# A MetaFormer block on one Trainium2 core: quarter-tile mixing, a column-tiled transform along w, unstrided scaling and one bias addition

## The chip, the cores and the metric

The kernel runs on one core of one Trainium2 chip. The metric is the device time of one execution in microseconds. The kernel before took 2752.03 us, the median of two runs (2751.84 and 2752.21 us).

## What is computed

The input x is 8 images of 128 x 128 points (h, w) with 96 channels, in fp32. One layer is applied to it:

```python
x = x + conv(_ln_c(x))            # layer norm over the 96 channels, then conv
t = x as tokens
t = t + ffn(_ln_t(t))             # layer norm again, then a quantised MLP
# conv(x), per image, with MED = 192 and a half spectrum of 128 x 65:
x_pre = scale * relu(x @ w1.T) ** 2 + bias
xf = rfft2(x_pre over h, w)                        # "ortho"
r = softmax over 3 filters of a small MLP of the image's means
comb = sum_s filt[s] * r[s]                        # complex, resized from small tables
out = irfft2(xf * comb) @ w2.T                     # 192 -> 96 channels
# ffn: 96 -> 384 -> 96, products in fp8 (5 exponent bits), sums rounded to fp16
y = q16(q8(x) @ q8(W1).T);  h = relu(q16(y + q8(b1)));  out = q16(q16(q8(h) @ q8(W2).T) + q8(b2))
```

## The kernel before, in words

Both Fourier transforms are matrix products. Work on image b is cut into three streams. Stream "a" (`before`, lines 622 to 827) goes over w in 32 units of 4 columns, and normalises, projects (96 to 192 + 48), rectifies, squares, transforms along h and stores the rows to DRAM. Stream "s" (`spectrum`, lines 829 to 1102) goes over 33 groups g of spectrum rows: it transforms along w, multiplies by the filter of the image, goes back to a real basis, mixes 192 channels into 96 for a pair p of groups, and inverts along w; there are 16 pairs. Stream "c" (`after`, lines 1104 to 1258) goes over w in 32 units again: last inverse transform along h, residual, layer norm, the fp8 MLP, output. Three images are in work at once, one in each stream.

The order of the instructions is fixed when the program is built. Every step is entered with `at(time, what, ..., after=..., banks=...)`: a time from tables written out by hand (`STREAMS`, `O`, `OWN`), the steps that it needs, and how many of six PSUM banks it takes. `in_order` (line 323) is a list scheduler that turns this into one order, and lines 1285 to 1295 pin each engine's instructions to it. So each engine, and each of the queues that issue DMAs (SP's and ACT's), works strictly in that order, and a step that is late holds up what stands behind it.

The steps that the change touches are these.

- **Scaling.** `load_xT` (644) brings 8 columns of x, transposed, as [96, h, 8]; `load_r` (652) brings 1/std as [h, 8], spread over 96 partitions; `scale` (656) multiplies 4 columns at a time into one of three buffers `zTs`, reading both inputs with a step of 8 elements. `project` (669) uses the result as stationary operand.
- **Transform along w.** `pack` (859) on POOL gathers the last 64 channels of two rows into one 128-column operand. `along_w` (868) then does three fp32 products of 128 rows x 128 columns against 130 columns; it is called twice for a group (cs = 0 and 1).
- **Filters.** `filters_of` (878) does twelve products of 52 rows x 64 columns, placed so that four lie in different quarters of TensorE's array; for the last group (g = 32) only the upper row half is used, six products.
- **Mixing.** `mix_low` (963) opens two banks with four bf16 products by zero (971), then adds sixteen 64 x 64 products for the third 64 channels (984). `mix` (992) adds eight 128 x 128 products (995). `mixed` and `invert` (1003, 1008) take the result out and transform it.
- **MLP.** `accumulated` (1174) copies 512 columns of a product to fp16 on ACT; `biased` (1179) adds b1 and clips at zero on DVE, once for each of three chunks; `hidden` (1183) casts all 1536 elements to fp8 on ACT.
- **Stream c's loads.** `load_v` (1112) brings x to a tile `xr`; `residual` (1127) writes the sum to a tile `t`, of which there are four.

Of the kernel before, what the change touches and what calls it, by code (L numbers as in the profile page):

```python
# [44 lines left out]
MED = 192  # L45
# [222 lines left out]
def _columns(p, r):  # L268

    if p < NP - 1:  # L270
        return [(g, cs) for g in (2 * p, 2 * p + 1) for cs in range(2)]
    return [(NG - 1, 0), (NG - 1, 1)] + [(NG, 0), (NG, 1)] * (r == 0) + [(NG + 1, 0)]
# [98 lines left out]
def metaformer_kernel(ctx: ExitStack, tc: tile.TileContext, a: dict, out: bass.AP):  # L371
    nc = tc.nc
    x, xT = a["x"], a["xT"]
# [49 lines left out]
    zeros = const.tile([128, 64], mybir.dt.bfloat16, name="zeros")  # L423

    NZT = 3
    zTs = [const.tile([C + 1, QW, 128], F32, name=f"zT{i}") for i in range(NZT)]
# [8 lines left out]
    w2A = load(T_CONST, "w2A", [128, C], a["w2T"][:128, :])  # L435
    w2B = const.tile([128, C], F32, name="w2B")
# [4 lines left out]
    b1q = const.tile([128, NHC], F32, name="b1q")  # L441
# [3 lines left out]
    def projection(sp):  # L445
# [36 lines left out]
        def others():  # L482
            for i in range(2):
                nc.sync.dma_start(out=w2B[64 * i : 64 * i + 64, :], in_=a["w2T"][128:, :])
            make_identity(nc, ident)
            nc.vector.tensor_copy(ident8, ident, saturate=False)
            nc.vector.memset(ones, 1.0 / (H * W))
            nc.vector.memset(zeros, 0.0)

            nc.vector.tensor_scalar(soa_bias, soa_bias, 128.0, None, ALU.mult)  # L490
# [6 lines left out]
    def filters(sp):  # L497
# [38 lines left out]
        def weights():  # L536
# [15 lines left out]
            nc.vector.tensor_copy(b1q, b1h)  # L552
# [69 lines left out]
    def before(b, t0, P):  # L622
# [4 lines left out]
        one = named("a", b, {None: NU, **dict.fromkeys(blocks, NWB), "load_xT": NU // 2, "load_r": NU // 2})  # L627
# [4 lines left out]
        def load_x(blk):  # L632
            if blk == 0:
                kept["gacc"] = pa.tile([C, NU], F32, name="gacc", tag="gacc")
            xb = pa.tile([128, WB, C], F32, name="xb", tag="xb")
            nc.sync.dma_start(out=xb, in_=x[b, :, blk * WB : (blk + 1) * WB, :])
            kept["x", blk] = xb
# [6 lines left out]
        def load_xT(hb):  # L644
            t = kept["xT", hb] = pa.tile([C, H, HB], F32, name="xT", tag="xT")
            nc.sync.dma_start(out=t, in_=xT[b, hb, :, :, :])

        def store_r(blk):
            t = kept["Rd", blk] = dram.tile([2, H, HB], F32, name="Rd", tag="Rd")
            nc.sync.dma_start(out=t.rearrange("f h w -> h f w"), in_=kept["r", blk].rearrange("h (f w) -> h f w", f=2))  # L650

        def load_r(hb):
            t = kept["rB", hb] = pa.tile([C, H, HB], F32, name="rB", tag="rB")
            nc.sync.dma_start(out=t, in_=kept["Rd", hb // 2][hb % 2].partition_broadcast(C))

        def scale(u):
            hb, q = divmod(u, 2)
            w = slice(q * QW, (q + 1) * QW)
            nc.vector.scalar_tensor_tensor(  # L659
                zTs[(b * NU + u) % NZT][:C, :, :],  # L660
                kept["xT", hb][:, :, w].rearrange("c h w -> c w h"),
                1.0,
                kept["rB", hb][:, :, w].rearrange("c h w -> c w h"),
                ALU.mult,
                ALU.mult,
                accum_out=kept["gacc"][:, u : u + 1],
            )

        def project(u, i0):
            px = kept["px", u, i0] = bank("px")[:, : 2 * (MED + SCTX)]  # L670
            for i in range(2):
                nc.tensor.matmul(  # L672
                    px[:, i * (MED + SCTX) : (i + 1) * (MED + SCTX)],
                    lhsT=zTs[(b * NU + u) % NZT][:, i0 + i, :],
# [42 lines left out]
        for u in range(NU):  # L717
            t = t0 + u * P
            blk, q = divmod(u, NQ)
            if q == 0:  # L720
# [3 lines left out]
                at(t + o["a_store_r"] * P, store_r, blk, after=[one("rest", blk)])  # L724
            if q % 2 == 0:
                hb = u // 2
                after = [one("scale", u - 4 + n) for n in (0, 1)]
                at(t + o["a_load_xT"] * P - 3, load_xT, hb, after=after)
                at(t + o["a_load_r"] * P, load_r, hb, after=after + [one("store_r", blk)])
            at(t + o["a_measure"] * P, measure, blk, q, after=[one("load_x", blk), one("rest", blk - 2)])  # L730
            after = [one("load_xT", u // 2), one("load_r", u // 2)] + both("project", u - NZT)
            at(t + o["a_scale"] * P, scale, u, after=after)
            for i0 in (0, 2):
                after = [one("scale", u), one("square", u - 2), one("context", u - 2)]
# [88 lines left out]
        after = [one("context", NU - 1), one("scale", NU - 1)]  # L823
# [5 lines left out]
    def spectrum(b, t0, P):  # L829
# [29 lines left out]
        def pack(g):  # L859

            yb = kept["yb", g] = psp.tile([128, 2, 2, 64], F32, name="yb", tag="yb")
            yt = kept["yt", min(g, NG)]
            src = yt[:, :, 128:].rearrange("w (s k) m -> w s k m", s=2)
            if g == NG:
                src = yt[:, 0:2, 128:].unsqueeze(2).to_broadcast([128, 2, 2, 64])
            nc.gpsimd.tensor_copy(yb, src)

        def along_w(g, cs):
            yt, yb = kept["yt", min(g, NG)], kept["yb", g]
            ja, jb = (2 * cs, 2 * cs + 1) if g < NG else (cs, cs) if g == NG else (2, 3)  # L870
            both = yb[:, 1 if g > NG else cs, :, :].rearrange("w k m -> w (k m)")
            pz = kept["pz", g, cs] = bank("pz")
            for u, y in enumerate((yt[:, ja, :128], yt[:, jb, :128], both)):
                nc.tensor.matmul(  # L874
                    pz[:, u * 2 * L : (u + 1) * 2 * L], lhsT=y, rhs=F2[:, cs, :], start=True, stop=True
                )

        def filters_of(g):
# [3 lines left out]
            halves = [(u, h, u * MED + 64 * h) for u in range(2) for h in range(2)]  # L882
            halves += [(2, k, k * MED + 128) for k in range(2)]
            for u, h, m0 in halves:
                for s in range(2 if g <= NG else 1):
                    p = slice(64 * s, 64 * s + R)
                    nc.tensor.matmul(  # L887
                        pf[64 * h : 64 * h + 64, s, u * 2 * L : (u + 1) * 2 * L],
                        lhsT=tb[p, m0 : m0 + 64],
                        rhs=RW[p, :],  # L890
                        start=True,
                        stop=True,
                    )
# [53 lines left out]
        def alone_t(g):  # L947
            z = kept["dm", g]
            nc.vector.tensor_tensor(z[:, 0, 0, 0:1], z[:, 0, 0, 0:1], soa_bias, ALU.add)
            nc.vector.tensor_tensor(z[:64, 2, 0, 0:1], z[:64, 2, 0, 0:1], soa_bias[:64], ALU.add)  # L950
# [12 lines left out]
        def mix_low(p):  # L963

            for r in range(2):
                kept["pv", p, r] = bank("pv")
            for h in range(2):
                for r in range(2):
                    half, rows = slice(64 * h, 64 * h + 64), slice(64 * r, 64 * r + 64)
                    n = len(_columns(p, r)) * C  # L970
                    nc.tensor.matmul(
                        kept["pv", p, r][half, :n],
                        lhsT=zeros[rows, :64],
                        rhs=zeros[rows, :1].to_broadcast([64, n]),
                        start=True,
                        stop=False,
                    )
            for i in range(5):
                for h in range(2):
                    for r in range(2):  # L980
                        if i < len(_columns(p, r)):
# [4 lines left out]
                                lhsT=kept["xf", g][rows, cs, 2, half],  # L986
                                rhs=w2B[rows, :],
                                start=False,
                                stop=False,
                            )  # L990

# [343 lines left out]
```

## Time and profile before

| what | value |
|---|---|
| two runs | 2751.84 and 2752.21 us |
| profiled execution: span from first to last instruction | 2754.4 us (no other time of this execution is recorded) |
| mean granted TensorE clock | 0.970 |
| PE / PEld / DVE / ACT / POOL busy | 93 / 71 / 83 / 81 / 77% of the span |
| DMA | 618.05 MB, mean 224 GB/s |
| PE, DVE, ACT, POOL busy from 500 to 1000 us | 492.16, 445.01, 429.79, 426.42 us |
| PE, DVE, ACT, POOL busy from 2610 to 2755 us | 88.57, 108.11, 123.78, 44.13 us |
| DVE: `biased` (L1181), 768 times | 427.5 us, 568 ns each |
| DVE: `scale` (L659), 256 times | 339.8 us, 1328 ns each |
| POOL: `pack` (L866), 264 times | 138.5 us, 525 ns each |
| ACT: `hidden` (L1185), 256 times | 386.2 us, 1509 ns each |
| DVE: bias of the second layer (L1207), 64 times | 67.4 us, 1054 ns each |

PE is TensorE's matmuls, PEld its weight loads, DVE the VectorE, ACT the ScalarE, POOL the GpSimd, SP a queue that issues DMAs. A group's line gives source line, engine, operation, "out<-in" by tile names, shapes, count, then busy time and the mean duration of one instruction. Busy time on PE is a union of overlapping instructions, so the start times of successive groups, in the timeline, say more on TensorE than busy time does. An fp32 product appears as two matmul records.

### The profile page before, as it was taken

What the parts mean: (1) busy time and instruction counts of PE and PEld (TensorE: products, weight loads), DVE (VectorE), ACT (ScalarE), POOL (GpSimd) and SP (SyncE); (2) the same over time, 40 slices, a digit from 0 to 9 for tenths busy, and PEclk for the clock granted to TensorE, in tenths of its full rate; (3) what the DMA queues carried; (4) which work ended last, traced back from release to release, by engine and by line L of the source; (5) the groups of instructions that cost most, each with busy time, mean ns of one, the idle gap of its engine ahead of it and who ended that gap; (6) DMA issues with size and microseconds to landing.
All of it is one profiled execution on the core that took longest, in us unless ns stands there. A gap on an engine that the chain in (4) does not pass through costs nothing.

```text
span 2754.4 us, 69406 instructions
## 1 busy us (share of the span) xinstructions
PE 2567.8 (93%) x25130; PEld 1953.0 (71%) x25130; DVE 2276.1 (83%) x5887; ACT 2233.0 (81%) x4452; POOL 2122.2 (77%) x3246
## 2 busy tenths in 40 slices
PE   4989999999999999999999999999999998999765
PEld 2668877777677777777677777777777776677433
DVE  3557667798898999889898889889889878999786
ACT  2665556699888879889998878889988997888898
POOL 1239997888788878988688969888788886889432
PEclk9899999999999999999999999999999998999896
DMA  7888777977688866878687757888777774656441
GB/s 205 263 263 253 242 224 241 287 233 251 209 255 260 252 213 196 271 242 262 220 258 245 243 171 220 273 259 257 231 239 242 230 222 147 185 178 190 149 129 62
DMA packets 480023, 618.05 MB, mean 224 GB/s; under 512 B 174542, under 2 KB 381270, under 8 KB 479658
## 3 DMA queue, kind: packets, MB, share of 16 engines
q1 hardware_dynamic: 424386, 462.60, 56.8%
q10 hardware_dynamic: 55296, 151.02, 14.7%
q8 instruction: 199, 3.26, 0.5%
q14 instruction: 142, 1.16, 0.1%
HBM read 405.36 MB, written 208.16 MB: 223 GB/s over the span
## 4 chain that ended last, share of the span: by engine, by line
PE 68%; DVE 13%; ACT 7%; POOL 4%; DMA 4%; issue 3%; SPq 1%; POOLq 0%; ACTq 0%; DVEq 0%
PE px L672 13%; PE pz L874 10%; PE py L701 10%; PE pv L995 7%; PE pf L887 6%; PE pg L1011 5%; PE ph L1170 4%; PE pk L1123 4%; PE po L1192 3%; PE pv L984 3%; DVE t L916 3%; DVE y L1181 2%; ACT h L1185 2%; ACT y L1177 2%; DVE st L581 2%
## 5 line engine op out<-in xcount | busy, mean ns | idle before, releaser
L923 POOL TENSOR_TENSOR rr<-t,t 128x390 f32<-128x390 f32 x512 | 520.4, 1017 | 60.4 <-DVE t L916 60.0
L672 PE MATMUL px<-W1S,zT 97*128 97x240 f32 x2048 | 519.4, 379 | 34.1 <-DVE zT L659 29.2
L1177 ACT CAST y<-ph 128x512 f16<-128x512 f32 x768 | 456.0, 603 | 24.2 <-PE ph L1170 22.4
L672 PEld LDWEIGHTS px<-W1S,zT 97*128 97x128 f32 x2048 | 377.2, 194 | 130.0 <-issue 33.7
L1151 ACT ACTIVATE z<-t,ln_m,ln_r 128x96 fp8e5<-128x96 f32 x960 | 461.2, 492 | 8.6 <-POOL ln_m L614 5.7
L1181 DVE TENSOR_SCALAR y<-y,b1q 128x512 f16<-128x512 f16 x768 | 427.5, 568 | 28.2 <-ACT y L1177 25.6
L683 ACT ACTIVATE rl<-px 128x480 f32<-128x480 f32 x512 | 295.7, 581 | 177.5 <-PE px L672 160.2
L701 PE MATMUL py<-X,F 128*128 128x384 f32 x1024 | 430.7, 507 | 2.1 <-ACT X L690 1.9
L1185 ACT ACTIVATE h<-y 128x1536 fp8e5<-128x1536 f16 x256 | 386.2, 1509 | 2.2 <-DVE y L1181 1.6
L659 DVE SCALAR_TENSOR_TENSOR zT<-xT,rB 96x512 f32<-96x512 f32 x256 | 339.8, 1328 | 53.1 <-DMA rB<-Rd 26.5
L874 PEld LDWEIGHTS pz<-F,yt 128*128 128x128 f32 x2080 | 301.4, 192 | 72.0 <-DVE t L1131 5.9
L1210 POOL TENSOR_TENSOR t<-t,o 128x1536 f32<-128x1536 f32 x64 | 210.1, 3282 | 167.8 <-DVE o L1207 165.8
L874 PE MATMUL pz<-F,yt 128*128 128x130 f32 x2080 | 329.0, 281 | 10.2 <-DVE t L1131 4.7
L857 POOL TENSOR_TENSOR tb<-tb,r 128x384 f32<-128x384 f32 (+1 forms) x264 | 287.0, 1087 | 59.7 <-DVE r L808 23.1
L916 DVE TENSOR_TENSOR t<-dm,pf 128x390 f32<-128x390 f32 x512 | 282.6, 552 | 43.8 <-PE pf L887 18.4
L1170 PE MATMUL ph<-zT,W1q 96*128 96x512 fp8e5 x768 | 293.5, 397 | 19.1 <-DVE zT L1166 13.9
L708 ACT COPY yst<-py 128x384 f32<-128x384 f32 x512 | 246.4, 486 | 74.3 <-PE py L701 67.8
L916 DVE TENSOR_TENSOR t<-dp,pf 128x390 f32<-128x390 f32 x512 | 280.3, 548 | 0.0
L940 POOL TENSOR_TENSOR xf<-rr 128x378 f32<-128x378 f32 x256 | 255.3, 997 | 19.7
L995 PEld LDWEIGHTS pv<-w2A,xf 128*128 128x128 f32 x2048 | 246.8, 194 | 13.6 <-issue 1.5
L995 PE MATMUL pv<-w2A,xf 128*128 128x96 f32 x2048 | 255.2, 278 | 0.0
L938 POOL TENSOR_TENSOR xf<-rr 128x390 f32<-128x390 f32 x256 | 250.1, 977 | 0.0
(126 smaller groups left out, 5210.5 us busy)
## 6 DMA issues: line engine op xcount, KB each, us to landing
Yd<-yst ACTq DMA_DIRECT2D x256, 384.0 KB
yt<-Yd SPq DMA_DIRECT2D x256, 384.0 KB
xb<-in_x SPq DMA_DIRECT2D x64, 768.0 KB
xT<-in_xT SPq DMA_DIRECT2D x128, 384.0 KB
rB<-Rd SPq DMA_DIRECT2D x128, 384.0 KB
tb<-T SPq DMA_DIRECT2D x256, 192.0 KB
Vd<-gst ACTq DMA_DIRECT2D x128, 384.0 KB
xr<-in_x SPq DMA_DIRECT2D x64, 768.0 KB
```

The costliest lines, as they stand in the source:

```text
L659: nc.vector.scalar_tensor_tensor(zTs[(b * NU + u) % NZT][:C, :, :], kept["xT", hb][:, :, w].rearrange("c h w -> c w h"), 1.0, kept["rB", h ...
L672: nc.tensor.matmul(px[:, i * (MED + SCTX) : (i + 1) * (MED + SCTX)], lhsT=zTs[(b * NU + u) % NZT][:, i0 + i, :], rhs=W1S, start=True, stop ...
L701: nc.tensor.matmul(py, lhsT=F1, rhs=kept["X", u][:, i0 : i0 + 2, :].rearrange("h w m -> h (w m)"), start=True, stop=True)
L874: nc.tensor.matmul(pz[:, u * 2 * L : (u + 1) * 2 * L], lhsT=y, rhs=F2[:, cs, :], start=True, stop=True)
L916: nc.vector.tensor_tensor(work(name, g), kept[d, g], pair(g, sign, c), ALU.mult)
L923: nc.gpsimd.tensor_tensor(kept["rr", g][:, :, 2 * i : 2 * i + 2, :], kept[ta, g], kept[tb, g][:, :, ::-1, :], op)
L995: nc.tensor.matmul(kept["pv", p, r][:, i * C : (i + 1) * C], lhsT=kept["xf", g][:, cs, r, :], rhs=w2A, start=False, stop=(i == len(_column ...
L1151: nc.scalar.activation(z, t, AF.Identity, bias=m, scale=r, saturate=False)
L1170: nc.tensor.matmul(kept["ph", u, n], lhsT=W1q[:, n * 128 : (n + 1) * 128], rhs=kept["zT", u], start=True, stop=True)
L1177: nc.scalar.copy(kept["y", u][:, n, :], kept.pop(("ph", u, n)))
L1181: nc.vector.tensor_scalar(y, y, b1q[:, n : n + 1], 0.0, ALU.add, ALU.max)
L1185: nc.scalar.activation(kept["h8", u], kept["y", u], AF.Copy, saturate=False)
```

## The change

1. **Mixing.** The eight 128 x 128 products and the four products by zero of a pair go. All of it is done in 64 x 64 products: 4 columns x 3 thirds of the channels x 2 x 2 quarters, 48 in all; `mix_low` does the first two columns (24), `mix` the last two. The last pair has 4 + 4 columns, where it had 5 + 3.
2. **Transform along w.** `pack` goes. `along_w` does six products of 128 rows x 64 columns, two for each third of the channels, one for each half of the output partitions. The filters and the spectrum take the same layout: 64 channels of two rows.
3. **Scaling.** x arrives from DRAM as [96, 8, h], straight in `zTs` (now four buffers of 8 columns), 1/std as [8, h]; one instruction of 1024 elements scales in place, without steps, for two units. The loads of x for the statistics and the store of 1/std get a layout in DRAM that fits.
4. **MLP.** b1 is spread to 1536 columns in fp16; one addition of 1536 elements takes the place of three of 512, and the clip at zero moves into the cast on ACT.
5. **Stream c.** x is loaded into the tile `t` (now five), the residual is added in place, and `load_v` waits for the store of the block five back.

The tables of times are not changed.

```diff
-    return [(NG - 1, 0), (NG - 1, 1)] + [(NG, 0), (NG, 1)] * (r == 0) + [(NG + 1, 0)]
+    return [(NG - 1, 0), (NG - 1, 1), (NG, r), (NG + 1, 0)]
...
-    NZT = 3
-    zTs = [const.tile([C + 1, QW, 128], F32, name=f"zT{i}") for i in range(NZT)]
+    NZT = 4
+    zTs = [const.tile([C + 1, HB, 128], F32, name=f"zT{i}") for i in range(NZT)]
...
-    b1q = const.tile([128, NHC], F32, name="b1q")
+    b1q = const.tile([128, NHC, QW * 128], F16, name="b1q")
...
         def load_xT(hb):
-            t = kept["xT", hb] = pa.tile([C, H, HB], F32, name="xT", tag="xT")
-            nc.sync.dma_start(out=t, in_=xT[b, hb, :, :, :])
+            nc.sync.dma_start(out=zTs[(b * NU // 2 + hb) % NZT][:C, :, :], in_=xT[b, hb, :, :, :])
...
-        def scale(u):
-            hb, q = divmod(u, 2)
-            w = slice(q * QW, (q + 1) * QW)
+        def scale(hb):
+            z = zTs[(b * NU // 2 + hb) % NZT][:C, :, :]
             nc.vector.scalar_tensor_tensor(
-                zTs[(b * NU + u) % NZT][:C, :, :],
-                kept["xT", hb][:, :, w].rearrange("c h w -> c w h"),
+                z,
+                z,
                 1.0,
-                kept["rB", hb][:, :, w].rearrange("c h w -> c w h"),
+                kept["rB", hb],
...
-                after = [one("scale", u - 4 + n) for n in (0, 1)]
+                after = both("project", u - 2 * NZT) + both("project", u - 2 * NZT + 1)
+                if b == 0:
+                    after.append((None, "make_weights"))
                 at(t + o["a_load_xT"] * P - 3, load_xT, hb, after=after)
...
-        def pack(g):
-
-            yb = kept["yb", g] = psp.tile([128, 2, 2, 64], F32, name="yb", tag="yb")
...
-            for u, y in enumerate((yt[:, ja, :128], yt[:, jb, :128], both)):
-                nc.tensor.matmul(
-                    pz[:, u * 2 * L : (u + 1) * 2 * L], lhsT=y, rhs=F2[:, cs, :], start=True, stop=True
-                )
+            first, step = (2 * cs, 1) if g < NG else (cs, 0) if g == NG else (2, 1)
+            for q in range(3):
+                for k in range(2):
+                    nc.tensor.matmul(
+                        pz[64 * k : 64 * k + 64, q * 2 * L : (q + 1) * 2 * L],
+                        lhsT=yt[:, first + step * k, 64 * q : 64 * q + 64],
+                        rhs=F2[:, cs, :],
...
+        def mix_part(p, columns):
+
+            for i in columns:
+                for q in range(3):
+                    for h in range(2):
+                        for r in range(2):
                             g, cs = _columns(p, r)[i]
                             half, rows = slice(64 * h, 64 * h + 64), slice(64 * r, 64 * r + 64)
                             nc.tensor.matmul(
                                 kept["pv", p, r][half, i * C : (i + 1) * C],
-                                lhsT=kept["xf", g][rows, cs, 2, half],
-                                rhs=w2B[rows, :],
-                                start=False,
-                                stop=False,
+                                lhsT=kept["xf", g][rows, cs, q, half],
+                                rhs=w2C[rows, q, :],
+                                start=(i == 0 and q == 0),
+                                stop=(i == 3 and q == 2),
                             )
 
+        def mix_low(p):
+            for r in range(2):
+                kept["pv", p, r] = bank("pv")
+            mix_part(p, (0, 1))
+
         def mix(p):
-            for r in range(2):
-                for i, (g, cs) in enumerate(_columns(p, r)):
-                    nc.tensor.matmul(
-                        kept["pv", p, r][:, i * C : (i + 1) * C],
-                        lhsT=kept["xf", g][:, cs, r, :],
-                        rhs=w2A,
-                        start=False,
-                        stop=(i == len(_columns(p, r)) - 1),
-                    )
+            mix_part(p, (2, 3))
...
-            xr = kept["xr", blk] = pools["c"].tile([128, WB, C], F32, name="xr", tag="xr")
+            xr = kept["t", blk] = pools["c"].tile([128, WB, C], F32, name="t", tag="t", bufs=5)
...
-        def biased(u, n):
-            y = kept["y", u][:, n, :]
-            nc.vector.tensor_scalar(y, y, b1q[:, n : n + 1], 0.0, ALU.add, ALU.max)
+        def biased(u):
+            y = kept["y", u]
+            nc.vector.tensor_tensor(y, y, b1q, ALU.add)
...
-            nc.scalar.activation(kept["h8", u], kept["y", u], AF.Copy, saturate=False)
+            nc.scalar.activation(kept["h8", u], kept["y", u], AF.Relu, saturate=False)
...
-                after = [one("residual", blk - 2, n) for n in range(NQ)] + [(("s", b), "store_v", p) for p in range(NP)]
+                after = [one("last", blk - 2, n) for n in range(NQ)] + [one("store", blk - 5)]
+                after += [(("s", b), "store_v", p) for p in range(NP)]
```

## The prediction

> **What bounds the kernel now.** I read the page's busy shares first, then the table of stages, then PE's timeline. The stages first (columns: length, then busy us of PE, PEld, DVE, ACT, POOL, then the granted clock and DMA):
>
> ```profile
> 500.00:1000.00 500.00, 492.16 (x4993) 380.93 (x4986) 445.01 (x1134) 429.79 (x873) 426.42 (x654) 1.00 0.80 247
> 1000.00:1500.00 500.00, 488.07 (x4813) 372.43 (x4816) 447.24 (x1159) 446.55 (x906) 417.44 (x634) 0.99 0.77 240
> 2610.00:2755.00 145.00, 88.57 (x645) 51.19 (x643) 108.11 (x326) 123.78 (x222) 44.13 (x92) 0.81 0.33 104
> ```
>
> In the bulk PE is busy 98% of the time, DVE 89%, ACT 88%, POOL 84%; only the end has ACT in front. Busy PE could still hide waits, so I took the start times from PE's timeline (start, length, group):
>
> ```profile
> 1205.51 0.61 PE L874 MATMUL pz<-F,yt 128*128 128x130 f32 x4
> 1205.95 0.39 PE L874 MATMUL pz<-F,yb 128*128 128x130 f32 x2
> 1206.18 0.61 PE L874 MATMUL pz<-F,yt 128*128 128x130 f32 x4
> ...
> 1211.64 0.38 PE L1170 MATMUL ph<-zT,W1q 96*128 96x512 fp8e5 x1
> 1211.95 0.36 PE L971 MATMUL pv<-zeros 64*64 64x384 bf16 x4
> 1212.13 0.83 PE L984 MATMUL pv<-w2B,xf 64*64 64x96 f32 x32
> 1212.89 0.42 PE L1156 MATMUL pz<-ident,z 128*96 128x128 fp8e5 x4
> 1213.15 1.98 PE L995 MATMUL pv<-w2A,xf 128*128 128x96 f32 x16
> 1214.97 0.40 PE L672 MATMUL px<-W1S,zT 97*128 97x240 f32 x1
> ```
>
> One `along_w` (6 records) takes 1206.18 - 1205.51 = 0.67 us from start to next start, `mix_low` with its zeros 1212.89 - 1211.95 = 0.94, `mix` 1.82. Start to start like this, each form keeps one pace throughout, for instance 0.669 us at the 25th percentile of 392 single `along_w`, 0.670 at the median. So PE issues back to back: the bulk is bound by TensorE, and any PE time added or removed there goes nearly whole into the span.
>
> **What a change of tile shape costs.** Between the records of two lines of full width, the start-to-start time exceeds the first's own pace by 0 ns (median of 2877 changes). From full width into the 64 x 64 products it is 93 ns (379 changes), and out of them 90 (383). In the lines above: `ph` needs 0.22 us, but the zeros come 0.31 after it. Two more views matter, since the change puts `along_w` on column tiles, which the kernel has hardly anywhere:
>
> ```profile
> 731.18 0.39 PE L874 MATMUL pz<-F,yb 128*128 128x130 f32 x2
> 731.50 0.88 PE L887 MATMUL pf<-RW,tb 52*64 52x130 f32 x12
> 732.31 0.39 PE L1170 MATMUL ph<-zT,W1q 96*128 96x512 fp8e5 x1
> ...
> 1615.98 1.92 PE L995 MATMUL pv<-w2A,xf 128*128 128x96 f32 x16
> 1617.84 0.25 PE L757 MATMUL pm<-ones,s 128*48 128x1 f32 x2
> 1618.01 0.71 PE L874 MATMUL pz<-F,yt 128*128 128x130 f32 x4
> ```
>
> The first is the last group's filter, six products that alternate between two column halves alone: 12 records in 0.81 us, six steps of 110.5 ns with two products in each, so column halves do run side by side. Its first step is 162 ns, not 110, and the exit costs 92. The second is a 128 x 48 product, the one form that already uses all rows and under 64 columns: the record before it comes 203 ns ahead, where L995's pace is 110, and the next line starts 112 ns after its last record. It pays about 90 ns each way too.
>
> **The Trainium skill.** "TensorEngine Tiling (Array Packing)", section Tiling Modes, lists 128 x 64 as two tiles and 64 x 64 as four, says that tiles run independently, and that changing the mode drains TensorE. The trace agrees: the drain is 90 to 93 ns each way. "Perfetto Trace Analysis", Identifying the Most-Contended Engine, warns that matmul busy share says little on headroom; hence start times here. "SBUF — State Buffer", Door 1: The DMA port swizzle, has lines of 16 bytes, so that fp32 reads 32 bytes apart each open a new one; `scale` at 1328 ns for 512 elements fits that. "GPSIMD Engine Reference", Specifications, says POOL shares SBUF interfaces with VectorE when that uses two ports or two SBUF inputs; L1181 runs from 253 to 3182 ns for one shape, which agrees.
>
> **The change part by part, on PE.**
>
> *Mixing.* Four quarters of 96 columns take 82.5 ns together (32 records of L984 in 0.66 us plus exit). Before, a pair costs zeros 0.187, L984 0.760 with its exit, L995 1.813 (median of 128): 2.760 us. After, 24 steps: 24 x 0.0825 = 1.980. Now `mix` also needs the quarter mode. In 42 of 128 pairs it follows `mix_low` directly: one first step (+0.051), one exit and spread (0.101), 2.132 us, a gain of 0.628. In 86 something lies between: two such extras and one more entry of 0.092, 2.376 us, a gain of 0.384. Sum: 42 x 0.628 + 86 x 0.384 = 59 us less.
>
> *Along w.* 392 single and 64 double runs, 456 in all (same order assumed). The template is the 0.815 us above (median of those column-pair runs), against 0.669, and an entry of 0.092: 0.146 + 0.092 = 0.238 us more per run, 108 us. Where a column-tile run lies next to a quarter-tile run (68 places, counted by giving the old order the new modes) one drain serves both: 68 x 0.091 = 6 less. So 102 us more.
>
> PE net: 102 - 59 = **+43 us** of work. Bounds: if 128 rows x 64 columns drained at no cost, -59; if the halves of 128-row weights didn't load in parallel, each step up to 2 x 0.11 us, +0.66 us for each of 520, 343 us more. The 128 x 48 record speaks against the first, the column pairs of the filter against the second; neither has both 128 rows and two halves, so I keep both ends.
>
> **The other engines.** *scale*: 256 x 1.328 + 20 us of accumulator reads become 128 instructions of 1024 elements. Nearest row: 390-element products take 552 ns, 576 elements 757, so about 1.1 ns an element plus 0.12: 1.25 us, 1.35 with the contention seen, 173 us. Gain 177 us (0 if the step isn't what costs). *biased*: 256 instructions like L1207 (same shape and type), 1.054 us: 270 against 427.5, gain 157; it could be 256 x 1.75 = 448 (L1207's longest), a loss of 20. *alone_t* and set-up: under 5. DVE: 2276 to about 1940. *pack*: POOL 138 us less. *ACT*: the cast keeps its 1.509 us, since the Relu from PSUM (480 elements, 581 ns) lies on the pace of the Copy (384, 486).
>
> These engines are hidden behind PE in the bulk, so their gain counts only through PE's waits. PE's time beyond pace and drains, in 20 slices of 138 us, is 4 to 6 us in quiet slices and 12 to 20 where an image's filter weights are worked out (a chain of small DVE steps behind other DVE work, lines 748 to 809). Summed over slices 2 to 17 it is 188 us; if all were quiet (5.3), 103 less. I take half, **-52**: DVE's queue gets a sixth shorter, ACT's does not, and what follows late there is ACT. At the end ACT sets the pace (124 of 145 us); I take -10 for start and end.
>
> **Waits added and moved.** `hidden` now waits for one addition after the third cast, not a third of it: about 0.5 us later per unit; behind it on ACT stand the next casts, and PE's `second` waits for it; the tables put 2 us between. `load_xT` waits for `project` of 8 units ago (57 us earlier in time than its use at -7 us, issued at -30) and no more for `scale`; SP's queue sees as many DMAs as before. In image 0 it waits for the weights, ready at some 12 us, while 1/std arrives only at about 40 (first `scale` at 41.6). `load_v` behind the store of five blocks ago: a tile lives about 16 of 20 unit lengths. `store_r` writes 64-byte pieces, 128 where there were 256. No cost for these; if a store were late, SP's loads behind it would wait, which is in the range.
>
> **Sum.** Against the profiled span 2754.4: +43 - 52 - 10 = 2735; the runs' median is 2.4 us under the span, so 2733.
>
> **The rivals.** *No relief* (15%): PE's waits come from ACT and from the order itself, which was timed for other durations. Speaks for it: ACT at 88% is untouched, and `po<-ACT h` is PE's longest wait, 34.6 us in total. Then 2752 + 43 = 2795, slower; it decides if less than 43 us of waits go. *Full relief* (20%): DVE was what made PE late; DVE chains stand in the critical chain at each image change, 14 us in one piece at 1011 to 1025. All slices quiet and 25 at the ends: 2752 + 43 - 103 - 25 = 2667. *Column tiles don't overlap* (5%): + 343 - 10, some 3080. The change then does the opposite of what it says; the filter's pairs speak against.
>
> **How the numbers follow.** The likeliest (60%) is 2733, own range 2700 to 2765. The range 2655 to 2810 holds it, full relief and no relief, and leaves out the serial tiles. About 2% (55 us) is what a measurement of this kernel can tell from no change: faster by that needs under 2697: full relief mostly, 0.2; slower, over 2807: serial tiles and the upper end of no relief, 0.1; within, 0.7.
>
> **What would show it.** `along_w` at 0.81 us from start to next start, with six steps of 110 ns, 92 ns entry; 0.0825 us per four quarters in both mixing steps; 1000 more drains of 90 ns; DVE at about 1940 us with `scale` near 1.3 and `biased` near 1.05; fewer PE waits in the slices at image changes. I am wrong if `along_w` takes 0.67 or 1.3, if `scale` stays at 2.6 us for 1024, or if PE's waits grow.

## The result and the profile after

The changed kernel takes **2819.82 us** (two runs, 2816.5 and 2823.14), against 2752.03: a ratio of 1.0235 (95% interval 1.021 to 1.0261). It is slower by 68 us, outside the predicted range. Its profiled execution has a span of 2814.6 us, 60.2 more than before, at a mean granted clock of 0.972 (before: 0.970), so the clock is not the cause.

First the page: busy time, the chain that ended last by engine (the work followed back from the last instruction, step by step, to what released it), and the new addition (busy us, mean ns | idle before, releaser).

```profile
PE 2623.4 (93%) x33882; PEld 1820.0 (65%) x33882; DVE 2039.5 (72%) x5110; ACT 2234.6 (79%) x4452; POOL 2057.3 (73%) x2983
...
PE 75%; ACT 7%; POOL 6%; DVE 4%; issue 3%; DMA 3%; SPq 1%; POOLq 0%; ACTq 0%; DVEq 0%
...
L1147 DVE TENSOR_TENSOR y<-y,b1q 128x1536 f16<-128x1536 f16 x256 | 289.9, 1132 | 52.9 <-ACT y L1143 52.5
```

DVE did get lighter, by 237 us, and the chain shows it: DVE's share fell from 13 to 4%. What took its place is not idle time but PE, from 68 to 75%. The table of stages says the same (length, then busy us of PE, PEld, DVE, ACT, POOL, then clock, DMA's share and GB/s):

```profile
500.00:1000.00 500.00, 495.54 (x6663) 347.44 (x6664) 382.29 (x967) 419.15 (x848) 396.98 (x579) 1.00 0.78 241
1000.00:1500.00 500.00, 487.93 (x6316) 337.97 (x6316) 388.14 (x978) 439.61 (x886) 397.28 (x570) 1.00 0.75 235
2610.00:2815.00 205.00, 128.62 (x950) 74.28 (x950) 141.40 (x337) 169.57 (x309) 68.26 (x126) 0.77 0.33 109
```

In the bulk PE is still busy 98 to 99% of the time, DVE only 76 to 78%. PE's timeline shows what it is busy with (start, length, group):

```profile
1202.00 0.89 PE L861 MATMUL pz<-F,yt 128*64 128x130 f32 x12
1202.82 1.08 PE L666 MATMUL px<-W1S,zT 97*128 97x240 f32 x4
...
1205.69 0.90 PE L878 MATMUL pf<-RW,tb 52*64 52x130 f32 x24
1206.52 1.08 PE L666 MATMUL px<-W1S,zT 97*128 97x240 f32 x4
1207.43 0.38 PE L1136 MATMUL ph<-zT,W1q 96*128 96x512 fp8e5 x1
```

`along_w` takes 1202.82 - 1202.00 = 0.82 us to the next start, as predicted (median of 390 single runs 0.816, predicted 0.815). The line to look at is `px` behind the filter's quarter tiles: 1207.43 - 1206.52 = 0.91 us from its start to that of `ph`, both of full width. In the kernel before, behind a product of full width, it was 0.81:

```profile
1208.07 0.98 PE L672 MATMUL px<-W1S,zT 97*128 97x240 f32 x4
1208.88 0.38 PE L1170 MATMUL ph<-zT,W1q 96*128 96x512 fp8e5 x1
```

This is no chance pair. Single runs of `px` that are followed by a line of full width take, after, 0.914 us in the median behind tiles (89 runs) and 0.812 behind full width (175); before, 0.914 (59) and 0.812 (305). For `py` it is 0.749 against 0.648. So the first fp32 product of full width behind tiles pays 0.10 us **on top of** the drain. The weight loads of the same two places show what goes with it, first after, then before:

```profile
1206.52 0.70 PEld L666 LDWEIGHTS px<-W1S,zT 97*128 97x128 f32 x4 [0.17 <-issue]
```

```profile
1207.75 0.92 PEld L672 LDWEIGHTS px<-W1S,zT 97*128 97x128 f32 x4
```

Before, `px` starts at 1208.07 and its first weights at 1207.75, 0.32 us ahead. After, both start at 1206.52: across the change of tiling nothing was loaded ahead, and the second record comes 307 ns behind the first in the median, where it is 207 behind full width. So it is throughout: at 439 changes of tiling into fp32 products of full width in the trace of after, the first weight load starts 2 ns ahead of its product in the median and never more than 31; between different products within full width it is 219 ns (1022 places). The Trainium skill, "TensorE: Matmul & The Clock Gate", Step-by-step: what each phase is for, says that TensorE pulls weight loads ahead of matmuls in flight; the trace agrees between products of one tiling, and shows the overlap missing at a change.

**An account of PE's span.** From the start times of all matmul records I added up: each record's own pace (what its form keeps in quiet stretches); what a change between tilings costs (drains); and the excess of the first step behind a change. What remains of the span is "rest": waits, stretches of lower clock and both ends. A figure in brackets is a count.

| us | before | after | change |
|---|---|---|---|
| own pace | 2290.5 | 2213.6 | -77 |
| drains (changes of tiling) | 86.2 (817) | 194.1 (1831) | +108 |
| first steps on tiles | 15.8 | 45.7 | +30 |
| first steps at full width | 23.9 (395) | 51.1 (816) | +27 |
| work, the sum | 2416 | 2504.5 | **+88** |
| rest | 338 | 310 | -28 |
| span | 2754.4 | 2814.6 | +60 |

The split depends on which stretches are taken as quiet. With the pace of a full-width form taken only from runs that stand between two other lines of full width, the work rises by some 80 us instead of 88.

### The profile page after: what moved, and what is told of

It is laid out like the page before. It is cut to its first block, busy times and chain, and to the rows that moved or that the text cites. A ratio compares the mean times of both kernels' runs of the same rounds, so it can differ in the third digit from the quotient of the medians.

```text
span 2814.6 us, 85810 instructions
## 1 busy us (share of the span) xinstructions
PE 2623.4 (93%) x33882; PEld 1820.0 (65%) x33882; DVE 2039.5 (72%) x5110; ACT 2234.6 (79%) x4452; POOL 2057.3 (73%) x2983
## 4 chain that ended last, share of the span: by engine, by line
PE 75%; ACT 7%; POOL 6%; DVE 4%; issue 3%; DMA 3%; SPq 1%; POOLq 0%; ACTq 0%; DVEq 0%
PE px L666 15%; PE pz L861 13%; PE py L695 12%; PE pv L962 9%; PE pf L878 6%; PE pg L984 5%; PE ph L1136 5%; PE pk L1093 4%; PE po L1158 4%; ACT y L1143 2%; POOL t L1176 2%; ACT h L1151 2%; PE pz L1122 2%; ACT z L1117 1%; POOL rr L915 1%
## 5 line engine op out<-in xcount | busy, mean ns | idle before, releaser
L915 POOL TENSOR_TENSOR rr<-t,t 128x390 f32<-128x390 f32 x512 | 531.3, 1046 | 102.3 <-DVE t L908 101.1
L666 PE MATMUL px<-W1S,zT 97*128 97x240 f32 x2048 | 525.7, 382 | 32.1 <-DVE zT L653 31.5
L861 PE MATMUL pz<-F,yt 128*64 128x130 f32 x6240 | 450.4, 283 | 8.9 <-DVE t L1099 5.2
L861 PEld LDWEIGHTS pz<-F,yt 128*64 128x64 f32 x6240 | 337.6, 137 | 167.1 <-issue 40.4
L695 PE MATMUL py<-X,F 128*128 128x384 f32 x1024 | 443.3, 520 | 0.9 <-ACT X L684 0.9
L853 POOL TENSOR_TENSOR tb<-tb,r 128x384 f32<-128x384 f32 (+1 forms) x264 | 302.6, 1146 | 78.2 <-DMA tb<-T 27.7
L1147 DVE TENSOR_TENSOR y<-y,b1q 128x1536 f16<-128x1536 f16 x256 | 289.9, 1132 | 52.9 <-ACT y L1143 52.5
L962 PE MATMUL pv<-w2C,xf 64*64 64x96 f32 x12288 | 309.3, 248 | 4.5 <-DVE t L1099 2.2
L962 PEld LDWEIGHTS pv<-w2C,xf 64*64 64x64 f32 x12288 | 268.7, 134 | 68.0 <-issue 29.1
L932 POOL TENSOR_TENSOR xf<-rr 128x378 f32<-128x378 f32 x256 | 263.3, 1028 | 19.7
L1099 DVE TENSOR_TENSOR t<-pk,t 128x384 f32<-128x384 f32 x256 | 141.0, 551 | 163.8 <-PE pk L1093 162.7
```

Source lines behind the costliest of these rows:

```text
L666: nc.tensor.matmul(px[:, i * (MED + SCTX) : (i + 1) * (MED + SCTX)], lhsT=zTs[(b * NU // 2 + u // 2) % NZT][:, QW * (u % 2) + i0 + i, :], ...
L695: nc.tensor.matmul(py, lhsT=F1, rhs=kept["X", u][:, i0 : i0 + 2, :].rearrange("h w m -> h (w m)"), start=True, stop=True)
L853: nc.gpsimd.tensor_tensor(kept["tb", g][p, :], kept["tb", g][p, :], rates[b][p, :], ALU.mult)
L861: nc.tensor.matmul(pz[64 * k : 64 * k + 64, q * 2 * L : (q + 1) * 2 * L], lhsT=yt[:, first + step * k, 64 * q : 64 * q + 64], rhs=F2[:, cs ...
L915: nc.gpsimd.tensor_tensor(kept["rr", g][:, :, 2 * i : 2 * i + 2, :], kept[ta, g], kept[tb, g][:, :, ::-1, :], op)
L962: nc.tensor.matmul(kept["pv", p, r][half, i * C : (i + 1) * C], lhsT=kept["xf", g][rows, cs, q, half], rhs=w2C[rows, q, :], start=(i == 0 ...
```

## The experiments

My theory: TensorE's added work, 88 us of changes of tiling and what follows them, makes the loss, and the relief of DVE is real but small (about 28 us of waits). The rivals: that the moved waits and the single addition make it (with TensorE as before, parts 3 to 5 would then be slower by themselves), or that `pack` mattered, or relief on POOL or DVE matters once the tiling costs are gone. Ratios are to runs of the kernel before on the same chip, beside each kernel. Parts are numbered as in the change.

**Parts 3 to 5 without TensorE's parts** (`light`): the kernel before with the unstrided scaling, the single addition and stream c's load into `t`; mixing, `pack` and `along_w` as before (parts 1 and 2 of the diff left out).

> The kernel before with parts 3 to 5 alone (scaling in place, one addition of b1, the load into t); pack, the transform along w and the mixing as before. Theory A (TensorE's drains and what follows them made the change slow; the relief of VectorE is real and small): PE's work is the same, about 28 us of waits go, some 2724 us. Rival B (the coarser scaling and the later single addition cost time themselves, TensorE only the 43 us that were predicted): 15 to 25 us slower than before, some 2770. Rival C (VectorE's relief is worth a lot and the tiles hid it): under 2690.

2767.39 us, ratio 1.0056 (1.0038 to 1.0074). So the three parts that were to bring the gain lose 15 us, where I had expected some 28 us less; the rival that they cost time themselves foretold it (some 2770). Work on PE is unchanged by the account (2416), the rest is 349 instead of 338.

**The transform along w at full width, without pack** (`full_w`): the changed kernel with every third channel as stationary operand.

```diff
-                        lhsT=yt[:, first + step * k, 64 * q : 64 * q + 64],
+                y = yt[:, first : first + 2, :].rearrange("w k m -> w (k m)")[:, q::3]
+                nc.tensor.matmul(to, lhsT=y, rhs=F2[:, cs, :], start=True, stop=True)
...
-                            lhsT=tb[p, m0 : m0 + 64],
+                            lhsT=tb[p, m0 : (k + 1) * MED : 3],
```

> The changed kernel, but along w every product has all 128 columns again, without pack: the stationary operand takes every third channel of two rows (a step of 3 elements), the filters and w2 are read in the same order. Only the one group per image that needs one row twice keeps column tiles (16 of 456 runs). Theory A: 440 excursions into column tiles go, each 0.146 us inside, 0.093 at the entry and about 0.06 in the first full-width product behind it, less some 8 us where they stood beside quarter tiles: 125 us less, some 2695. Rival B: only 0.24 us an excursion, 100 us less, some 2720. If the weight load pays for the step, up to 0.05 us for each of 3024 records' loads, 150 us more: no gain.

2850.68 us, 1.0358 (1.0328 to 1.0389): worse than the changed kernel. It has 1017 changes of tiling instead of 1831, but the strided weights cost more than those. One line of its weight loads (min/median/max ns), and the same of the kernel `packed_bias3` below, which reads them in a row:

```profile
L863 PEld LDWEIGHTS pz<-F,yt x3024: 251/260/335, 189.0 to 2635.7; 128*128 128x128 f32 x189
```

```profile
L870 PEld LDWEIGHTS pz<-F,yb x3120: 186/191/338, 192.9 to 2519.4; 128*128 128x128 f32 x195
```

A record of this form then comes every 164 ns instead of 112: a single run of six records takes 0.98 us to the next start in the median, where the kernel before needs 0.67. 3024 x 52 ns is 157 us more, against the 125 us that the changes of tiling were expected to return. The run doesn't refute the theory, but it isn't the clean "no column tiles" that it was meant to be.

**Mixing in one step** (`mix_once`): one visit to the quarter mode instead of two.

```diff
         def mix_low(p):
...
-            mix_part(p, (0, 1))
...
         def mix(p):
-            mix_part(p, (2, 3))
+            mix_part(p, (0, 1, 2, 3))
```

> The changed kernel with the mixing of a pair in one step of 48 products instead of two of 24. Theory A: 86 excursions into quarter tiles go, 0.161 + 0.093 + 0.06 us each, 27 us less, some 2793. If drains are hidden in waits anyway: no change, 2820.

2803.75 us, 1.0185 (1.0148 to 1.0223): 153 fewer changes of tiling, 24 us less work in the account, 14 less in the span. The direction is the theory's, but the two intervals overlap, and the changed kernel has only two runs: by itself this doesn't show a gain.

**Both** (`full_w_mix_once`):

> Both edits together. Theory A: 125 + 27 us less than the changed kernel, some 2668, under the kernel before by 3%. If waits on ScalarE take up what TensorE gives back, it stays above 2700.

2844.47 us, 1.0332 (1.0302 to 1.0362). The strided weights dominate it; it tells nothing new.

**The single addition apart** (`light_bias3`): `light` with the three additions of before, and the clip at zero back on DVE; only parts 3 and 5 remain.

```diff
-            nc.vector.tensor_tensor(y, y, b1q, ALU.add)
+            nc.vector.tensor_scalar(y, y, b1q[:, n : n + 1], 0.0, ALU.add, ALU.max)
...
-            nc.scalar.activation(kept["h8", u], kept["y", u], AF.Relu, saturate=False)
+            nc.scalar.activation(kept["h8", u], kept["y", u], AF.Copy, saturate=False)
```

> The kernel before with parts 3 and 5 alone: scaling in place and the load into t, but three additions of b1 with the clip on VectorE, as before. In the run with parts 3 to 5 the bulk ran 6 us ahead of the kernel before and the last 490 us lost 17. Theory A (the single addition, which waits for the third cast, makes the end longer, where only one image is left to fill in): the 17 us come back, some 2745. Rival B (the new loads of stream c or the scaling in units of eight columns cost it): stays at 2765.

2743.82 us, 0.9966 (0.9952 to 0.9981). So parts 3 and 5 gain 9 us, with 150 us less on DVE; part 4 alone turns that into a loss of 15. It costs 25 us (0.0090 x 2752), although its instructions are cheaper. These are they in `light` and in `light_bias3` (min/median/max ns):

```profile
L1177 DVE TENSOR_TENSOR y<-y,b1q x256: 894/959/2604, 542.9 to 2752.5; 128x1536 f16<-128x1536 f16 x128
```

```profile
L1177 DVE TENSOR_SCALAR y<-y,b1q x768: 251/428/3179, 540.1 to 2733.4; 128x512 f16<-128x512 f16 x192
```

Most of it is lost at the end. From the last `px` of image 7 to the last `po` it takes 479.9 us in the kernel before, 479.8 in `light_bias3`, and 496.6 in `light`. The chain that ended last, in order of time, shows one block of stream c there (pieces called "issue", under 0.1 us, left out); first `light`, then `light_bias3`:

```profile
2649.86 3.11 POOL t L1206
...
2665.21 0.97 ACT y L1173 x2
2666.21 0.96 DVE y L1177
2667.17 0.24 DVE z L1145
2667.41 0.88 DVE o L1203
2668.36 3.11 POOL t L1206
```

```profile
2653.25 3.11 POOL t L1206
...
2669.16 0.55 ACT o L1199
2669.72 0.97 DVE o L1203
2670.77 3.11 POOL t L1206
```

In `light` the addition waits for the third cast (L1173), and the block's own bias `o` (L1203) stands behind it on DVE; POOL's sum, and the next block's statistics, wait for `o`. With three additions `o` starts right behind its producer on ACT. From one sum to the next it is 18.50 us against 17.52.

The single addition does one thing more: GpSimd gets slower beside it. The pages of `light` and `light_bias3` have the same 3247 instructions on POOL, and 142 us between them:

```profile
PE 2572.3 (93%) x25130; PEld 1955.4 (71%) x25130; DVE 2046.1 (74%) x5119; ACT 2232.6 (81%) x4452; POOL 2185.6 (79%) x3247
```

```profile
PE 2561.9 (93%) x25130; PEld 1950.5 (71%) x25130; DVE 2126.4 (77%) x5631; ACT 2233.1 (81%) x4452; POOL 2043.3 (74%) x3247
```

The medians of POOL's forms are nearly the same in both (`rr` 949 ns), so I took each instruction's excess over its form's median (forms with 64 or more). The 346 that overlap the single addition in time exceed it by 536 ns on average, the 972 that overlap one of the three additions by 65 ns, and all the others by 36 ns in both kernels. POOL's share of the chain that ended last is 9% in `light` and 3% in `light_bias3`.

**The single addition, but three in the last two images** (`light_end3`):

```diff
+            if b < B - 2:
+                added = [one("biased", u)]
...
+            else:
+                added = [one("biased_n", u, n) for n in range(NHC)]
```

> Parts 3 to 5, but in the last two images the b1 addition is done in three pieces, as before. Theory A (the single addition costs only at the end, where one image is left and VectorE's queue waits for the third cast): the 20 us between 2767 and 2744 come back, 2740 to 2748. Rival B (it costs everywhere, through later casts): 2755 or more.

2754.5 us, 1.0007 (0.9999 to 1.0015). Of the 25 us between `light` and `light_bias3` this returns 13. In its profile the stretch from the last `px` to the last `po` is back to 481.9 us, so the end is mended, and what is left should lie ahead of it. Where is open: the last `px` starts at 2260.9 us, against 2256.6 in `light_bias3`, and executions of one kernel differ by as much. POOL is still busy for 2177 us in this run, with 8% of the chain. The slower GpSimd may make this rest, but no run tests it, and in the changed kernel 107 us more of POOL's time cost nothing (`dead_pack` below).

**The changed kernel with three additions** (`after_bias3`): the same edit on the kernel after.

> The changed kernel with three additions of b1 again. Theory A: 9 to 17 us less than the changed kernel, 2803 to 2811, since its end lost 9 us against the kernel before. Rival B: 2820, or more, as VectorE gets 137 us of work back.

2806.84 us, 1.0194 (1.0178 to 1.0211). Here the single addition costs some 11 us (the two intervals just touch), and TensorE's parts 1 and 2 (against `light_bias3`) cost 0.0228 x 2752 = 63. They are the main cause: 63 and 11, less the 9 that parts 3 and 5 gain, make 65 of the 68 us.

**Gathering instead of column tiles** (`packed_bias3`): `after_bias3`, but GpSimd gathers all 192 channels of two rows into [third, row, 64], and `along_w` does three products of full width on it. The filters and the mixing stay in the new layout.

```diff
+                    src = yt[:, 2 * s : 2 * s + 2, :].rearrange("w k (q m) -> w q k m", q=3)
+                nc.gpsimd.tensor_copy(yb[:, s if g <= NG else 0, :, :, :], src)
...
+                    lhsT=yb[:, cs, q, :, :].rearrange("w k m -> w (k m)"),
```

(shown for the ordinary group; the last row, which stands twice, has its own case.)

> The last one, with the operand of the transform along w gathered on GpSimd for all 192 channels (two copies of 384 elements a group), so that the products have all 128 columns, side by side in memory, and no column tiles are left. Theory A (drains and the first products behind them): 456 excursions of 0.146 + 0.093 + 0.06 us go, 125 to 135 us less than after_bias3, some 2680; GpSimd goes from 2057 to some 2380 us busy. Rival B (only the 43 us of the prediction's sum are TensorE's): 70 us less at most. Rival C (GpSimd becomes late with the copies): PE waits for yb, and it stays above 2750.

2731.34 us, 0.9923 (0.9907 to 0.9938). Column tiles instead of gathering, with the same mixing, cost 0.0271 x 2752 = 75 us. I had expected 125 to 135, as the account has it (133 us less work). Against `light_bias3`, which mixes as before, it is 12 us faster, with 46 us less work in the account: so much the new mixing brings here, beside larger copies on GpSimd; the sum had 59 us of work. Its page, and what PE waits for because of the added copies (us, times, longest):

```profile
PE 2516.5 (92%) x30762; PEld 1870.0 (69%) x30762; DVE 2150.4 (79%) x5622; ACT 2217.2 (81%) x4452; POOL 2202.4 (81%) x3503
```

```profile
PE pz L870 <- POOL yb L864: 7.7, 9, 2.1
```

POOL is busy for 2202 us with the 520 copies of some 507 ns, and PE's products wait for them only 7.7 us in all, its weight loads 18.8 (22 times).

**The same with mixing in one step** (`packed_once_bias3`):

> And the mixing in one step of 48. Theory A: 86 excursions into quarter tiles less, 16 to 27 us under packed_bias3 (the changed kernel gained 16 from this edit), some 2660.

2729.69 us, 0.9917 (0.9901 to 0.9933): the fastest here, and faster than both kernels. From `packed_bias3` it can't be told apart, where 16 to 27 us had been expected.

**The drains by themselves** (`drains`): `light_bias3`, with a product of one column on 128 rows x 48 columns ahead of every second transform along h. 256 of them; no result is used.

```diff
+            if i0 == 0:
+                nc.tensor.matmul(full[:48, 400:401], lhsT=F1[:, :48], rhs=ones, start=True, stop=True)
```

> light_bias3 (2744 us) with one product of 128 rows x 48 columns against a single column ahead of every second transform along h, 256 in all, its result unused. It does next to no work, but TensorE has to change its tiling twice, and nothing else in the kernel changes. Theory A (each costs 92 ns at the entry, about 0.07 for its two passes, 0.09 at the exit, and then some 0.1 us because the second weight load of the full-width product behind it isn't ready): 0.35 us each, 90 us of TensorE's time, and the bulk gives two thirds of it to the span: 50 to 90 us slower, some 2815. Rival B (only the drains that the prediction counted, 0.25 us, and as much again hidden in waits): under 35 us, below 2780.

2815.04 us, 1.0229 (1.0215 to 1.0243), against 0.9966 without them: 0.0263 x 2752 = 72 us, 0.28 each, for products that stream one column. The work in the account rises by 74, the span by 69. The place in PE's timeline:

```profile
1203.66 0.81 PE L1126 MATMUL pk<-vin,GK 128*128 128x384 f32 x2
1204.40 0.25 PE L701 MATMUL py<-ones,F 128*48 128x1 f32 x2
1204.58 0.91 PE L702 MATMUL py<-X,F 128*128 128x384 f32 x2
1205.33 0.61 PE L877 MATMUL pz<-F,yt 128*128 128x130 f32 x4
```

`pk` needs 0.65 us but the tiny product starts 0.74 behind it: 0.09 of drain. `py` then starts 0.18 later, and takes 0.75 instead of 0.65. So a visit to another tiling (in and out again) can be priced from this line: about 0.09 in, 0.09 out, 0.10 for the first product of full width behind it; the other 0.09 are the tiny product's own two passes. That makes 0.37 us here, of which 0.28 reach the span on average (30 of the 256 stand beside another tiling, and save a change). This is the piece of the theory that is **shown**: next to no work but changes of tiling was added, and most of their time came out in the span. A tiny product of full width, which would show the passes alone, was not run.

**The gathering on VectorE** (`packed_dve`): `packed_once_bias3`, with the 520 copies on DVE.

```diff
-                nc.gpsimd.tensor_copy(yb[:, s if g <= NG else 0, :, :, :], src)
+                nc.vector.tensor_copy(yb[:, s if g <= NG else 0, :, :, :], src)
```

> packed_once_bias3 (2730) with the gathering on VectorE instead of GpSimd. TensorE's work there is 158 us less than in after_bias3 (drains, first products), but the span only 86 less: the rest went into other waits. Theory A1 (GpSimd at 81% with 277 us of copies is what is late): 10 to 30 us less, some 2710. Theory A2 (ScalarE, the most loaded of the others in the bulk, or the fixed order, is late next): within 10 us of 2730. Rival: VectorE's copies lock GpSimd out and it gets slower.

2770.74 us, 1.0073 (1.0058 to 1.0089): 43 us slower (0.0156 x 2752) than the same copies on POOL. First its page, then the wait that stands out on POOL, then the same wait with the copies on POOL (`packed_once_bias3`):

```profile
PE 2518.1 (91%) x30762; PEld 1880.2 (68%) x30762; DVE 2335.1 (85%) x6142; ACT 2219.5 (80%) x4452; POOL 1945.1 (70%) x2983
```

```profile
POOL rr L924 <- DVE t L917: 118.0, 92, 7.6
```

```profile
POOL rr L924 <- DVE t L917: 26.2, 18, 6.7
```

DVE at 85% delays those who wait for it, and its share of the chain that ended last goes from 7 to 20%. GpSimd's own instructions are not longer for it (`rr` 1006 ns against 999), so the expected rival, that DVE's copies lock GpSimd out, isn't seen. So DVE's load is not without meaning: taking 150 us off 2276 gains 9, putting 175 on 2160 costs 43.

**The old copies back, unused** (`dead_pack`): `after_bias3` with `pack` on GpSimd as it was before, ahead of `along_w` in the order; its result isn't read.

```diff
+            nc.gpsimd.tensor_copy(yb, yt[:, :, 128:].rearrange("w (s k) m -> w s k m", s=2))
```

> after_bias3 (2807) with pack put back on GpSimd at its old place in the order, its result unused: 264 copies of 256 elements, 138 us of GpSimd's time. After_bias3 has 87 us more of TensorE's time than light_bias3 but took only 61 us longer. Theory A (the missing 26 us are the relief of GpSimd, which lost pack): 20 to 30 us slower than after_bias3, some 2832. Rival B (they are waits that went to nothing because TensorE was later anyway): within 8 us of 2807.

2805.07 us, 1.0205 (1.0182 to 1.0228), against 2806.84 and 1.0194: the 128 us of copies on POOL that part 2 removes are worth nothing that these runs can tell.

## Why the prediction was wrong, step by step

**Right in mechanism and size.** The bulk is bound by TensorE, and work added there goes largely into the span. `along_w`: 0.816 us, predicted 0.815; column halves of 128 rows do run side by side, so the rival of serial tiles is out. Mixing: 1.151 us for a single step of 24 products, predicted 1.142; 2.143 for the 41 double ones, predicted 2.132. Changes of tiling: 1014 more, predicted some 1000. The queues: PE's wait for scaled x, the one behind which loads stand, went from 29.2 to 31.5 us only.

Against the span, -19 was predicted and +60 came. Of the 79 us between them 45 lie in TensorE's work, 34 in the rest (with the other choice of paces some 36 and 43).

**Wrong, first: the cost of a change of tiling, +43 where it is +88.** The sum had an entry and an exit of 90 to 92 ns, and a first step on the tiles. It missed that the first fp32 product of full width *behind* tiles pays another 0.10 us: +27 in the account. The drains came to +108 rather than 93 (1014 changes at 106 ns instead of 92; the account counts small waits at a change with them), +15. The trace of before had it already, 59 `px` of 0.914 us beside 305 of 0.812; I took the median pace for the form's pace and put this excess (23.9 us in the run) with the waits on other engines.

**Wrong, second: "I take half, -52", and "-10 for start and end".** Little of this came from a lighter DVE: 9 us at most. The experiments give that to parts 3 and 5, which lighten POOL by 79 us as well and move stream c's loads, and parts 3 to 5 together a loss of 15; the rival "no relief" (2795) is the nearest. Two things failed. Slices in which PE waits more were laid to DVE because its small chains stand there; DVE's chains did go out of the chain that ended last, but the time didn't. And PE's own longest waits hardly moved:

```profile
PE px L666 <- DVE zT L653: 31.5, 10, 12.4
PE po L1158 <- ACT h L1151: 31.3, 33, 2.3
```

Before, these were 29.2 and 34.6 us. Both stand at points where DVE's length isn't what is late: all 50.2 us of DVE's idle time ahead of `zT` are ended by DMA, and `h` is ACT's.

**Wrong, third: the wait that was priced at nothing.** "`hidden` now waits for one addition after the third cast ... about 0.5 us later per unit ... No cost for these". What stood behind the longer wait was not ACT's `hidden` but DVE's own `o`, and with it POOL's sum and the next block. The cover is PE, and near the end it is gone: in the last 205 us PE is busy for 129. From the last `px` on, `light` loses 17 us. The kernel after loses 9 (488.8 against 479.9), of which some 6 go with the single addition: `after_bias3` has 483.2. That the addition also slows GpSimd had no term in the sum. The prediction had read the spread of `biased`, 253 to 3182 ns, as DVE and POOL getting into each other's way, but counted it on DVE alone; on POOL the single addition adds 120 us here (2057.3 against 1937.8 in `after_bias3`). What those cost in time isn't shown.

**DVE's own figure.** 1940 was predicted, 2039.5 came. `biased` is 1132 ns on average (predicted 1054), `scale` 1440 (1350): as rows these two fell by 304 us with their accumulator reads, not 334. But rows can't be taken off busy time: successive instructions overlap on DVE, and the rows of before add up to 2542 us where the busy time is 2276. Of the 304 us, 237 arrived.

**What stays open.** By and large the rest falls as the work rises:

| kernel | PE work, us | rest, us | span, us |
|---|---|---|---|
| packed_once_bias3 | 2345 | 376 | 2720.9 |
| packed_bias3 | 2370 | 356 | 2725.8 |
| light_bias3 | 2416 | 330 | 2745.6 |
| mix_once | 2480 | 321 | 2800.9 |
| drains | 2490 | 325 | 2814.7 |
| after_bias3 | 2503 | 304 | 2806.8 |

Between the first and the last, 158 us of work move the span by 86: a slower TensorE meets fewer late partners. That this is what the rest is made of is argued from the table, not shown; and why the drains come out nearly one to one (+74, +69) and the column tiles don't (-133, -81) I can't say. Part of that gap is the account's own: with the other choice of paces the work is some +86 and -122, so that four fifths and two thirds of it reach the span. `dead_pack` only excludes that the gap is POOL's relief.

## What to carry to other kernels

Before moving a product to tiles to save a copy or to fill the array, count the visits, not the products: here each visit cost some 0.28 us of the span (in, out, and a first product of full width without its weights loaded ahead), and two copies a group on an engine with room were far cheaper than the visits that they saved. An engine's busy time that is hidden is worth what it delays, not what it weighs: 150 us off DVE gave 9 at most, and one longer wait ahead of a short instruction that others need took 17. Look also at what a new form does to the engine beside it: the addition that took DVE less time took GpSimd 142 us more. Where start-to-start times are used as a form's pace, split them by what stood ahead before calling the excess a wait.

## What the runs showed of the hardware that I had not expected

- Behind a change of tiling the first fp32 record of `px` takes 307 ns to the next, where it takes 207 within full width; the first weight load is never more than 31 ns ahead there (439 places), and 219 ns in the median within full width.
- A product of 128 rows x 48 columns that streams a single column, put ahead of a product of full width 256 times, costs 0.28 us of the span each.
- A stationary fp32 operand read with a step of three elements loads in 260 ns instead of 191, and the records' pace goes from 112 to 164 ns.
- fp16 bias on DVE: 512 columns with one scalar per row take 251 ns at best, 428 in the median and up to 3179; 1536 columns against a full tile 894, 959 and 2604.
- GpSimd's instructions that overlap this addition against a full tile take 536 ns more than their form's median on average (346 in `light`); beside the additions with one scalar per row it is 65 ns (972 in `light_bias3`).
